# Bank of one transpose, a rounding piece and a search operation in a retention and FFN kernel

## The chip, the cores and the metric

The kernel runs on one core of one Trainium2 chip. The metric is device time in microseconds (us), the median of several executions; lower is better. The core has five engines with queues of their own: TensorE (PE, with its weight loads as PEld), VectorE (DVE), ScalarE (ACT), GpSimd (POOL) and SyncE (SP, which here only sends transfers).

## The reference

The input x has 4 sequences of 1024 tokens of 512 features, all float32. The computation is one layer in two parts, each added to its input after a layer norm on both sides:

```python
# part 1: x1 = x + layernorm(attn(layernorm(x)))
lam = clip(1.0 - 2.0 ** -beta, tiny, 1.0 - 1e-09)          # one per head, 16 heads of 32
q = (x @ Wq.T).reshape(B, L, 16, 32)
v = (x @ Wv.T).reshape(B, L, 16, 32)
ret = scan over time: state = lam * state + v_t
out = (q * ret).reshape(B, L, 512)
out = layernorm(out) * gamma + beta_ln
out = (out * silu(x @ Wg.T)) @ Wo.T
# part 2: out = x1 + layernorm(ffn(layernorm(x1))), inner width 1536
w_q = w.astype(float8_e4m3fn).astype(float32)              # for gate_w, up_w, down_w
gate = silu((x @ gate_wq) * gate_scale)
up = (x @ up_wq) * up_scale
out = ((gate * up) @ down_wq) * down_scale
```

The FFN weights are rounded to float8 and multiplied as float32.

## The kernel before

The 4096 tokens are cut into 8 blocks of 512 tokens (`TB`), a block into 4 tiles of 128 tokens. `Retention(t)` holds part 1 of block t, `Ffn` part 2. The FFN of a block runs in 12 steps (`NI`), one for each 128 of the 1536 inner columns. The main loop (`for t in range(NB)`, line 800) goes over blocks and, inside, over steps `i`. In iteration t it works on the FFN of block t (`f`, from `a`), on part 1 of block t + 1 (`b`, spread over the steps), on the beginning of block t + 2 (`n`, from step 4 or so), and on the end of the FFN of block t - 1 (`l`). All engine instructions are kept in the order in which the program names them, by the wrapper `InOrder` (its call is line 74, so every instruction of a profile shows line 74). Nothing reorders them: each engine runs its own list in that order, and semaphores between engines come from the tiles that instructions share.

[...] Two belong to the pool "pa" (products of part 1: pv, pq, pg, po, the means mu and var, and turns, named pt), two to "pf" (gate's and up's products in the FFN, pfg and pfu), four to "pd0" to "pd3" (the sums of down). A pool with two buffers hands them out in turn; a new tile has to wait until the last reader of the tile two places before it is done.

Three places matter.

Step 11, `if n and i == 11` (line 892). It holds the start of block t + 2 and the end of part 1 of block t + 1: `n.v(0)` makes pv (8 matmul instructions), `n.scan(0)` runs the scan over it on DVE (tile ret), `b.turn_x1n(3)` transposes the normalized x1 of the last tile by four matmuls into a bank (pt), and `b.upper_of(3)` and later `b.rest_of(3)` split it into two float32r parts, x1nT, one on ACT, one on DVE. Then `n.q(0)` makes pq (line 947), and `n.y_of(0)` multiplies it by ret on DVE. Tiles 0 to 2 are transposed otherwise, on DVE and by transfers through DRAM (`move_x1n`). The next iteration's `f.gate(0)` reads all of x1nT.

Rounding of the FFN weights. In float32, 18 pieces of 128 x 1024 elements are rounded during the prologue and block 0's FFN by `round_weights` (line 183), a generator; `rounds(n)` takes n of its operations. For each piece they are: a mask of the exponent on DVE (`unit`), two ACT instructions on the result, and an add and a subtract on DVE (`finish`). The add of a piece comes after the mask of the next one. The two ACT instructions are not sent with the mask, but at the next `units()`, which flushes all masks that are open; `rounds` calls it after each operation unless it is given `now=False`, and `finish` calls it when its own piece is still open. After its subtract, a piece frees its scratch, and the load of a later piece goes out on SP. In block 0's FFN three operations (one piece) run at step 0's beginning, three at step 4's beginning and three after `f.up` and `f.fuse` of each of the steps 0 to 7; the flush is before `f.up`, and in step 3 also right after `f.gate` and after each operation.

The variance of part 1's layer norm. In step 3 of an iteration, `b.halves()` splits the sum of y over the chunks into a float32r upper half on ACT and a lower half on DVE, `b.g_of(0)` makes pg, `b.mean()` averages both halves over the partitions on PE (mu), and `b.center_y()` subtracts mu from y on DVE, four instructions, squares the four results on ACT and sums the squares on POOL (sqsum). In step 4 the same halves are made of sqsum and averaged on PE (var), behind `b.g_of(1)`. Then come a square root on ACT and, after `f.up` and `f.fuse`, a reciprocal on DVE.

The search. `find_over` (line 228) is a generator of 24 ACT instructions that look for weights outside float8's range; each reads a quarter of one of the three weight matrices (128 x 1536) with one sign and writes a tile seen and its sum. From the seventh on, seen is one of two buffers that the halves and squares above use too. The table `look` (line 798) says how many run in each step of iteration t = 1: half of them, rounded down, after `f.gate`, and the others after `f.up` and `f.fuse`.

Of the kernel before, what the change touches and what calls it, by code (L numbers as in the profile page):

```python
# [23 lines left out]
def retention_ffn_sandwich(  # L24
# [190 lines left out]
    def units():  # L215

        while open_units:
            _, c = open_units.pop(0)
            act.activation(c, c, AF.Relu, bias=neg_low)
            act.activation(c, c, AF.Identity, scale=1.5 * 2.0**20, bias=low_unit)  # L220

    def rounds(n, now=True):
        for _ in range(n):
            next(rounding, None)
            if now:
                units()
# [71 lines left out]
    def turn(src, name, home="pa"):  # L298
        pt = homes[home].tile([P, NC, P], F32, tag=home, name=name)
        for c in range(NC):  # L300
            pe.transpose(pt[:, c, :], src[:, ts(c, P)], ident)
        return pt
# [14 lines left out]
    class Retention:  # L317
# [204 lines left out]
            )  # L522
            self.pt = {}

        def turn_x1n(self, s):
            self.pt[s] = turn(self.x1n.pop(s), f"pt1_{self.t}_{s}")

        def move_x1n(self, s):

# [160 lines left out]
    b = Retention(1)  # L690
# [104 lines left out]

    look = [2, 2, 2, 0, 2, 3, 3, 2, 2, 2, 2, 2]
    l = None
    for t in range(NB):  # L800
        f, n = Ffn(a), None
        for i in range(NI):
            if t > 0 and (t > 1 or i):
                (f if i else l).rest((i - 1) % NI)
            if t == 0 and i == 0:
                n = Retention(2)
                rounds(3, now=False)
            if t == 0 and i == 4:
                rounds(3, now=False)

            if l and i == 0:
# [25 lines left out]
            if t == 0 and i in (5, 6):  # L837
                n.norm_x(2 * i - 10, True)
                n.norm_x(2 * i - 9, True)
            if i == 3:  # L840
                units()
            for _ in range(look[i] // 2 if t == 1 else 0):
                next(search)

# [8 lines left out]
                l.stats(1)  # L853
            if b and i == 3:
                b.halves()
                b.g_of(0)
                b.mean()
                b.center_y()
                if t == 0:
                    n.stats(3)  # L860
                    n.rstd()
                    n.shift()
# [29 lines left out]
            if n and i == 11:  # L892
                n.v(0)
                n.scan(0)
                b.turn_x1n(3)
                b.upper_of(3)
            if t == 0:
                if i < 8:
# [66 lines left out]
        l, a, b = f, b, n  # L965
# [70 lines left out]
```

## Time and profile before

| | us |
|---|---|
| median of 3 runs (lowest, highest) | 1018.53 (1018.28, 1019.45) |
| the profiled execution | 1021.44 |
| its span, first to last instruction | 1019.7 |
| PE busy | 995.2 |
| DVE busy | 635.3 |
| ACT busy | 328.3 |
| POOL busy | 242.6 |
| PE matmuls of pfu, pfg and pd | 217.2, 190.2, 189.3 |
| PE matmuls of pq, pg, po | 115.5, 114.8, 114.5 |

The busy time of an engine is the sum over its instructions; the ends of matmuls are modelled, so that groups of matmuls overlap a little in the timeline. A row of the waits names the engine that stood still, the tile that it was about to write and the engine and tile that released it. A line of the timeline has the start from the beginning of the span, the length, the engine, the operation, output and inputs, how many instructions are merged in it, and in brackets the idle time before it with its releaser. Block numbers are not in the tile names: a place is found by its time. The FFN of block 0 begins at about 96 us, and an iteration of the loop takes about 123 us.

### The profile page before, as it was taken

The page shows a single profiled execution, that of the slowest core. Times are in us where ns is not written, and L with a number is a line of the kernel's source. Part 1 is how long each engine was busy: PE and PEld are TensorE (multiplying, and loading weights), DVE is VectorE, ACT ScalarE, POOL GpSimd, SP SyncE. Part 2 cuts the span into 40 slices and gives each one's busy share as a digit, 9 for nine tenths or more (in the row PEclk, how much of TensorE's full clock was granted, in tenths as well). Part 3 has the DMA queues.
Part 4 walks back from the last instruction along what each step waited for, and adds up shares of the span by engine and source line. Part 5 has one row for each costly group of instructions (what it writes and reads, how often), then busy time and mean ns, then how long its engine had stood idle before and what let it go on. Part 6 is the DMA issues. An engine that isn't in the chain of part 4 may idle for free.

```text
span 1019.7 us, 9800 instructions
## 1 busy us (share of the span) xinstructions
PE 995.2 (98%) x3502; PEld 654.1 (64%) x3502; DVE 635.3 (62%) x945; ACT 328.3 (32%) x489; POOL 242.6 (24%) x290
## 2 busy tenths in 40 slices
PE   8999989999999999999999999999999999999997
PEld 7454656656666666666666566665666656666885
DVE  4996888436767277663767537674476735747444
ACT  3546555523755124111231113211142111412222
POOL 1405131302222032221413114131141302313021
PEclk9999989999999999999999999999999999999999
DMA  8312212500216004250022501134020510103021
GB/s 283 120 62 88 98 63 82 135 11 21 62 56 171 1 22 144 78 150 1 21 73 83 134 1 58 35 114 104 0 83 31 129 68 1 42 21 123 2 83 41
DMA packets 62608, 73.79 MB, mean 72 GB/s; under 512 B 5856, under 2 KB 36320, under 8 KB 62560
## 3 DMA queue, kind: packets, MB, share of 16 engines
q1 hardware_dynamic: 60976, 72.24, 23.2%
q10 hardware_dynamic: 1584, 0.94, 0.4%
q8 instruction: 27, 0.44, 0.2%
q14 instruction: 21, 0.17, 0.1%
HBM read 43.53 MB, written 29.62 MB: 72 GB/s over the span
## 4 chain that ended last, share of the span: by engine, by line
PE 91%; DVE 4%; POOL 2%; ACT 1%; issue 1%; DMA 1%; ACTq 0%; POOLq 0%; DVEq 0%
PE pfu L74 17%; PE pfg L74 17%; PE pd L74 17%; PE pv L74 11%; PE pq L74 10%; PE po L74 10%; PE pg L74 9%; DVE ret L74 1%; DVE scr L74 1%; DMA x<-in_x 1%; POOL sqsum L74 1%; POOL x L74 0%; PE var L74 0%; POOL mv L74 0%; PE mu L74 0%
## 5 line engine op out<-in xcount | busy, mean ns | idle before, releaser
L74 PE MATMUL pfu<-x1nT,up_sb 128*128 128x512 f32 x768 | 217.2, 425 | 0.0
L74 PE MATMUL pfg<-x1nT,gate_sb 128*128 128x512 f32 x768 | 190.2, 390 | 1.1 <-ACT x1nT L74 0.7
L74 PE MATMUL pd<-down_sb,fuse 128*128 128x512 f32 x720 | 189.3, 405 | 0.0
L74 PEld LDWEIGHTS pfu<-x1nT,up_sb 128*128 128x128 f32 x768 | 145.6, 190 | 56.1 <-issue 28.9
L74 PEld LDWEIGHTS pfg<-x1nT,gate_sb 128*128 128x128 f32 x768 | 143.9, 188 | 31.7 <-DVE x1nT L74 1.0
L74 PEld LDWEIGHTS pd<-down_sb,fuse 128*128 128x128 f32 x720 | 136.0, 189 | 38.4 <-issue 10.8
L74 ACT CAST fuse<-gate 128x512 fp32r<-128x512 f32 x90 | 55.7, 619 | 274.9 <-DVE gate L74 274.9
L74 ACT ACTIVATE gate<-pfg,gs_sb 128x512 f32<-128x512 f32 x96 | 65.9, 687 | 234.3 <-PE pfg L74 234.2
L74 DVE SCALAR_TENSOR_TENSOR gate<-pfu,us_sb,gate 128x512 f32<-128x512 f32 x96 | 71.8, 748 | 106.3 <-PE pfu L74 106.2
L74 PE MATMUL pq<-xnT,wq_sb 128*128 128x512 f32 x256 | 115.5, 594 | 5.5 <-DVE ret L74 5.5
L74 PE MATMUL pv<-xnT,wv_sb 128*128 128x512 f32 (+1 forms) x280 | 114.8, 556 | 1.8 <-ACT xnT L74 1.8
L74 PE MATMUL pg<-xnT,wg_sb 128*128 128x512 f32 x256 | 114.8, 592 | 0.0
L74 PE MATMUL po<-wo_sb,y 128*128 128x512 f32 x256 | 114.5, 592 | 0.0
L74 POOL TENSOR_SCALAR mv<-mv 128x1 f32<-128x1 f32 (+1 forms) x77 | 19.8, 257 | 318.7 <-DVE mv L74 318.1
L74 PEld LDWEIGHTS pv<-xnT,wv_sb 128*128 128x128 f32 x280 | 52.8, 189 | 48.8 <-issue 43.4
L74 PEld LDWEIGHTS pq<-xnT,wq_sb 128*128 128x128 f32 x256 | 47.8, 189 | 55.9 <-issue 47.4
L74 DVE TENSOR_TENSOR fuse<-gate,fuse 128x512 fp32r<-128x512 f32 x90 | 79.4, 883 | 6.9 <-ACT fuse L74 6.9
L74 PEld LDWEIGHTS po<-wo_sb,y 128*128 128x128 f32 x256 | 48.4, 189 | 50.1 <-issue 47.7
L74 PEld LDWEIGHTS pg<-xnT,wg_sb 128*128 128x128 f32 x256 | 48.3, 189 | 49.6 <-issue 47.0
L74 POOL TENSOR_TENSOR x<-x,x1n 128x512 f32<-128x512 f32 x32 | 49.1, 1534 | 45.4 <-DVE x1n L74 35.5
L74 DVE TENSOR_TENSOR_SCAN ret<-lam,pv 128x512 f32<-128x512 f32 x16 | 19.5, 1219 | 54.4 <-PE pv L74 54.4
L74 DVE BATCH_NORM_STATS2 st<-x 128x6 f32<-128x512 f32 x64 | 43.6, 681 | 14.9 <-POOL x L74 11.2
(112 smaller groups left out, 926.1 us busy)
## 6 DMA issues: line engine op xcount, KB each, us to landing
kept<-x SPq DMA_DIRECT2D x32, 256.0 KB, 2.1
x<-kept SPq DMA_DIRECT2D x32, 256.0 KB, 4.0
x<-in_x SPq DMA_DIRECT2D x28, 256.0 KB, 4.1
out<-d SPq DMA_DIRECT2D x27, 256.0 KB, 2.0
xnT<-mx SPq DMA_DIRECT2D x24, 256.0 KB, 4.7
mxs<-xs SPq DMA_DIRECT2D x84, 64.0 KB, 1.8
x1n<-mxs SPq DMA_DIRECT2D x21, 256.0 KB, 2.6
mx<-xn SPq DMA_DIRECT2D x20, 256.0 KB, 2.2
```

The lines of the kernel that those rows point to most:

```text
L74: return lambda *args, **kwargs: tc.keep_in_program_order(op(*args, **kwargs))
```

## The change

It does three things.

1. `turn_x1n` takes the pool of its bank as an argument, and the call in step 11 under `if n` (iterations 0 to 5) uses "pf". The other calls keep "pa".
2. In block 0's FFN the three rounding operations from the beginning of step 4 go to step 3, behind `b.halves()`. The flush `units()` of step 3 (which stood behind `f.gate`, before `b.halves()`) goes to the same place, between them.
3. In `look`, step 4 has one operation in place of two, and step 7 three in place of two. In step 4 that is the one behind `f.gate`, in step 7 one more behind `f.fuse`.

```diff
-        def turn_x1n(self, s):
-            self.pt[s] = turn(self.x1n.pop(s), f"pt1_{self.t}_{s}")
+        def turn_x1n(self, s, home="pa"):
+            self.pt[s] = turn(self.x1n.pop(s), f"pt1_{self.t}_{s}", home)
...
-    look = [2, 2, 2, 0, 2, 3, 3, 2, 2, 2, 2, 2]
+    look = [2, 2, 2, 0, 1, 3, 3, 3, 2, 2, 2, 2]
...
             if t == 0 and i == 0:
                 n = Retention(2)
                 rounds(3, now=False)
-            if t == 0 and i == 4:
-                rounds(3, now=False)
...
-            if i == 3:
-                units()
             for _ in range(look[i] // 2 if t == 1 else 0):
                 next(search)
...
             if b and i == 3:
                 b.halves()
+                units()
+                if t == 0:
+                    rounds(3, now=False)
                 b.g_of(0)
                 b.mean()
                 b.center_y()
...
             if n and i == 11:
                 n.v(0)
                 n.scan(0)
-                b.turn_x1n(3)
+                b.turn_x1n(3, "pf")
                 b.upper_of(3)
```

`turn` is unchanged; it already takes the pool:

```python
    def turn(src, name, home="pa"):
        pt = homes[home].tile([P, NC, P], F32, tag=home, name=name)
        for c in range(NC):
            pe.transpose(pt[:, c, :], src[:, ts(c, P)], ident)
        return pt
```

## The prediction

> **What bounds the kernel now.** I read the busy table, the chain that ended last, the waits of TensorE, and then three stretches of the timeline. TensorE is the bound:
>
> ```profile
> PE 995.2 (98%) x3502; PEld 654.1 (64%) x3502; DVE 635.3 (62%) x945; ACT 328.3 (32%) x489; POOL 242.6 (24%) x290
> ...
> PE 91%; DVE 4%; POOL 2%; ACT 1%; issue 1%; DMA 1%; ACTq 0%; POOLq 0%; DVEq 0%
> ```
>
> So a change pays only where PE stands still. The waits (engine, waited for, us in total, times, longest) name two rows inside the loop, and the change touches both:
>
> ```profile
> PE pq L74 <- DVE ret L74: 5.5, 6, 1.0
> PE var L74 <- DVE half L74: 4.4, 2, 3.7
> ```
>
> The first sits in step 11 of blocks 0 to 5. Timeline, end of block 0 (start, length, engine, tile; in brackets the idle time before it):
>
> ```profile
> 204.19 0.60 PE L74 MATMUL pt<-ident,x1n 128*128 128x128 f32 x4
> ...
> 204.40 1.22 DVE L74 TENSOR_TENSOR_SCAN ret<-lam,pv 128x512 f32<-128x512 f32 x1 [2.61 <-PE pv L74]
> ...
> 205.67 3.70 PE L74 MATMUL pq<-xnT,wq_sb 128*128 128x512 f32 x8 [0.88 <-DVE ret L74]
> ```
>
> pv, pt and pq are consecutive users of the two "pa" banks: pq needs pv's bank, and the scan still reads it. The second row has one wait of 3.73 us in step 4 of block 0 and one of 0.68 us in step 4 of block 1:
>
> ```profile
> 131.49 1.22 DVE L74 TENSOR_TENSOR gate_sb<-scr,scr 128x1024 fp32r<-128x1024 f32 x1
> ...
> 132.08 0.61 ACT L74 CAST half<-sqsum 128x512 fp32r<-128x512 f32 x1
> ...
> 136.23 0.68 DVE L74 TENSOR_TENSOR half<-sqsum,half 128x512 fp32r<-128x512 f32 x1
> ...
> 136.97 0.80 PE L74 MATMUL var<-half,mean_r 128*128 128x512 f32 x1 [3.73 <-DVE half L74]
> ...
> 137.56 3.62 PE L74 MATMUL pfu<-x1nT,up_sb 128*128 128x512 f32 x8
> ```
>
> In block 0 the upper half was ready at 132.69, but DVE finished one weight piece, took the rest of fuse_3 and rounded another piece before the lower half. The pfu group behind it took 3.62 us where others take 1.98: the clock in one-microsecond windows is 0.64 in 136 to 137, 0.50 up to 143, 0.94 in 143 to 144.
>
> [...] after the 0.68 us gap (pfu 2.02 us) nothing fell. [...] during POOL's sqsum sums a scr sum took 2.29 us in place of 1.22. [...]
>
> **Part 1, the turn (blocks 0 to 5).** No instruction is added; two dependences change. pt takes the bank of pfg_11, read by ACT until 323.74 in block 1, where pt starts at 328.10: no wait. pq_0 takes the bank of po_3, read last at 320.28 to 321.09: no wait. The gain of a site is the time from pt's end to pq's end, less eight unstalled f32 matmuls, 3.43 us by the chain: 209.37 - 204.79 - 3.43 = 1.15 us in block 0. In blocks 1 to 5 it is 1.26, 1.15, 1.21, 1.15 and 1.21 [...]. The sum is 7.13. In block 6 pt is followed by pd without a wait, and pd ends 1.86 after pt where eight unstalled take 1.83: some 0.03 per site remains. I take **-7.0**, bounds -5.5 (the bare idle) and -7.2.
>
> What is late next? gate_0 of the next block needs all of x1nT; in block 1 DVE finishes it at 331.04, and gate_0 starts at 335.08, so 333.8 when all moves up: 2.8 us of cover, 2.8 to 3 in blocks 2 to 5 too (577.19 against 581.23, less 1.2). up_0 takes pt's bank, free from that same DVE instruction, and starts at 339.92. v(1) takes pv_0's bank, free at 329.64, wanted at 335.7. y_of(0) on DVE follows pq, 1.2 earlier, and DVE is idle there (2.39 before it). If the cover failed, every microsecond beyond 2.8 would stall PE one for one.
>
> **Part 2, the search operation (block 1).** ACT's order was gate_4, seen, half[...]:
>
> ```profile
> 259.98 1.56 ACT L74 ACTIVATE seen<-gate_sb,neg_max 128x1536 fp8e4<-128x1536 f32 x1
> 261.44 0.19 ACT L74 ACTIVATION_READ_ACCUMULATOR seen<-gate_sb,neg_max 128x1 f32 x1
> 261.53 0.61 ACT L74 CAST half<-sqsum 128x512 fp32r<-128x512 f32 x1
> ```
>
> Without the seen pair the cast can start at 260.22, when POOL's sqsum (256.04 plus 4.14) is done; it ends at 260.83. The lower half then waits for the first of POOL's two d sums (260.14 to about 261.5) and ends near 262.1; that it gets in between two POOL sums is seen at 257.00, where two DVE operations took 2.04 us during POOL's three sqsum sums. pg_1's matmuls end at 262.78, so nothing waits. From var's start to pfu's took 264.03 - 262.22 = 1.81; in step 3, mu without a wait takes 253.75 - 252.88 = 0.87. Gain **-0.9**; bounds -0.95 and 0 (if the half waits for both d sums, until 263.08, it ends where it did). rstd stays at 264.73 behind the table load (263.44 plus 1.28), but reciprocal follows gate_4 on DVE, which moves up with pfu.
>
> In step 7 the operation (1.57 plus 0.19) goes behind the one at 294.14; gate_8 on ACT moves from 296.39 to 297.6. Its reader on DVE starts at 301.72, and pfg_8's bank is wanted at 303.26: covered by 3 us. xs of step 8 (298.88) takes the buffer of the added seen, finished at 297.6: covered by 1.2 us, and behind it by x1nT's slack. Cost 0.
>
> **Part 3, the rounding piece (block 0).** It moves three DVE instructions (0.68, 1.22, 1.22) ahead of center_y in step 3, and with them the flushes of ACT. Its load is out at 115.81 and lands in 3.6, before 122.8. The instruction that SP sends after each piece (piece 15's load) goes out near 127 in place of 132.74, earlier; nothing queues behind it.
>
> DVE is free at 122.26, the half of ysum is ready since ACT no longer flushes first (cast at 119.8 instead of 122.03): lower half 122.26, piece 122.86 to 125.9, center_y at 125.86 where it was at 123.94, 1.9 later. mu comes 0.4 earlier, which PE only spends waiting for var. POOL's first sqsum sum ends 3.4 after center_y (ACT's last sq started at 127.35 against 123.94): that sq at 129.27.
>
> Now ACT's new order decides: sq, flush of piece 13, fuse_3, **flush of piece 14**, gate_4, half. Flush 14 ran after rstd before (138.39); now it stands ahead of the half. By start-to-start times in the trace: sq 0.56, flush 2.23, fuse 0.54, flush 2.23, gate 0.57: half at 129.27 + 6.13 = 135.40, done at 136.0. DVE, free by 135.4, makes the lower half until 136.7; var's second matmul starts at about **136.8**, where it was 136.97. So the piece leaves DVE's queue ahead of the half, but ACT's queue gets as long as DVE's was: the 3.7 us wait stays, now mostly for the upper half. Gain 0.2. PE starts again with var's first matmul at 136.05, 0.9 earlier, so the half-clock stretch may end a little earlier. I take **-0.4**; bounds -4 ([...] 6 us at half speed cost 3.0) and +3 [...]. rstd comes at 138 in place of 137.80 and is needed at 141.9.
>
> **Sum.** -7.0 - 0.9 - 0.4 = **-8.3**. The profiled execution took 1021.44 with a span of 1019.7: its span becomes 1011.4. The median is 2.9 under the profiled time; its waits should be the same, so 1018.53 - 8.3 = **1010.2**.
>
> **Rivals.**
> - *The clock falls differently in block 0.* [...] 3.0 more go: 1007.2. For: PE resumes 0.9 earlier by a first matmul. Against: idle stays about 3.7. The reverse gives 1013.2.
> - *Part 3 works as its DVE side suggests*: the half directly after sqsum (132.3), wait and slow clock gone: 3.73 + 3.0 in place of 0.4, near 1003.9. [...]
> - *The turn only exchanges its wait*: half of 7.0, for instance because gate_0 waits for x1nT, 1013.7. Against: 2.8 us of cover in each block.
> - *Slower*: ACT takes x1nT's tile 2 only when its DMA has landed (574.11 in block 3, ACT idle 4.11). If that landed over 2.8 + 8.3/6 = 4.2 us later in all six blocks, gate_0's stall would eat everything; at 5 us the time is 1023. Against: nothing on SP ahead of it is moved there.
> - *The change doesn't do what it says*: the order of instructions shows it does, ACT's flushes included.
>
> **How the numbers follow.** Main case 0.68 (1008.8 to 1011.6); the clock better 0.13, worse 0.05; part 3 as hoped 0.03; an exchanged wait 0.07; no change 0.02; slower 0.02. Cutting the ends leaves 1006.8 to 1012.9. Below 0.2% (2.0 us) a measurement cannot tell a change; faster 0.96, same 0.02, slower 0.02.
>
> **What would show it.** Right: the row pq waiting for ret is gone; in each of blocks 0 to 5 pq ends some 3.5 after pt; only one gap before var is left, 3.5 to 4.2 us in block 0, with ACT's flush of piece 14 between fuse_3 and gate_4; center_y there near 125.9. Wrong: a new row for pfg or pt in step 11, or var's gap in block 0 under 2 us or over 5.

## The result, and the profile after

| | before | changed |
|---|---|---|
| median of 6 runs (lowest, highest), us | 1018.78 (1018.28, 1019.45) | 1010.83 (1010.38, 1011.77) |
| the profiled execution, us | 1021.44 | 1010.72 |
| its span, us | 1019.7 | 1008.9 |
| PE idle (span less busy), us | 24.5 | 17.5 |

The ratio is 0.9923 with a 95% interval of 0.9910 to 0.9936, so 7.95 us less by the medians. The two profiled executions differ by more, 10.8 us in span, and two things in that are not the change. Before starts its first pv at 11.16 us, the changed kernel at 9.62, because the first loads of x landed at different times (the one on the way to that pv took 5.67 us in before and 4.11 in the changed kernel). And the half-clock stretch in block 0 is of different length in the two (below): from var's second matmul to the pfg behind it takes 6.85 us in before (136.97 to 143.82) and 5.59 in the changed kernel (135.06 to 140.65), a difference of 1.3 us. So places are compared here by distances inside an execution, not by their times from the start.

The busy table and the chain by engine, of the changed kernel, answer to the first two lines of before: TensorE is still the bound.

```profile
PE 991.4 (98%) x3502; PEld 652.7 (65%) x3502; DVE 633.8 (63%) x945; ACT 328.0 (33%) x489; POOL 241.2 (24%) x290
...
PE 91%; DVE 3%; POOL 2%; ACT 2%; DMA 1%; issue 0%; ACTq 0%; SPq 0%; POOLq 0%; DVEq 0%
```

TensorE's waits (us in total, times, longest) that answer to the two rows of before:

```profile
PE var L74 <- ACT half L74: 3.6, 1, 3.6
...
PE pv L74 <- DMA xnT<-mx: 0.2, 1, 0.2
PE var L74 <- DVE half L74: 0.2, 1, 0.2
```

The row of pq waiting for ret (5.5 us, 6 times) is gone. Of the 4.4 us in which var waited for the half of VectorE, 0.2 are left, but 3.6 have come in which it waits for the half of ScalarE. A small row is new: a pv that waits for the transfer of xnT.

The timeline of step 11 at the end of block 0, changed kernel: pq now starts right behind the turn (201.48, where the turn starts at 201.04), while the scan still reads pv's bank, that is, pv's buffer of 128 x 512 float32.

```profile
201.04 0.60 PE L74 MATMUL pt<-ident,x1n 128*128 128x128 f32 x4
201.24 1.22 DVE L74 TENSOR_TENSOR_SCAN ret<-lam,pv 128x512 f32<-128x512 f32 x1 [2.61 <-PE pv L74]
201.48 3.60 PE L74 MATMUL pq<-xnT,wq_sb 128*128 128x512 f32 x8
```

And steps 3 and 4 of block 0, changed kernel, from center_y to pfu_4:

```profile
124.20 2.47 DVE L74 TENSOR_TENSOR y<-y,mu 128x512 f32<-128x512 f32 x4
...
127.60 0.63 ACT L74 ACTIVATE sq<-y 128x512 f32<-128x512 f32 x1 [0.80 <-POOL sqsum L74]
...
128.14 1.13 ACT L74 ACTIVATE scr<-scr,neg_low 128x1024 f32<-128x1024 f32 x1
...
129.31 1.15 ACT L74 ACTIVATE scr<-scr,low_unit 128x1024 f32<-128x1024 f32 x1
...
130.36 0.60 ACT L74 CAST fuse<-gate 128x512 fp32r<-128x512 f32 x1
...
130.87 1.14 ACT L74 ACTIVATE scr<-scr,neg_low 128x1024 f32<-128x1024 f32 x1
...
132.05 1.15 ACT L74 ACTIVATE scr<-scr,low_unit 128x1024 f32<-128x1024 f32 x1
...
133.10 0.67 ACT L74 ACTIVATE gate<-pfg,gs_sb 128x512 f32<-128x512 f32 x1
133.67 0.60 ACT L74 CAST half<-sqsum 128x512 fp32r<-128x512 f32 x1
...
134.31 0.69 DVE L74 TENSOR_TENSOR half<-sqsum,half 128x512 fp32r<-128x512 f32 x1 [0.74 <-ACT half L74]
134.33 0.50 PE L74 MATMUL var<-half,mean_r 128*128 128x512 f32 x1 [3.58 <-ACT half L74]
...
135.06 0.52 PE L74 MATMUL var<-half,mean_r 128*128 128x512 f32 x1 [0.22 <-DVE half L74]
...
135.39 3.57 PE L74 MATMUL pfu<-x1nT,up_sb 128*128 128x512 f32 x8
```

ScalarE runs without a pause from the last square to the upper half: flush of piece 13, fuse_3, flush of piece 14, gate_4, half. VectorE is now the one that waits (0.74 us). The last line shows half clock again behind the gap (pfu took 3.57 us, in step 3 of the same block 2.00). How long it lasted is read from windows of one microsecond (start and end, length, busy time and count of PE, PEld, DVE, ACT, POOL, then the granted clock, the share of the DMA engines and GB/s). These are the first and the last window of the stretch, in before:

```profile
136.00:137.00 1.00, 0.03 (x1) 0.03 (x1) 0.91 (x2) 0.00 (x0) 0.37 (x1) 0.64 0.00 0
...
143.00:144.00 1.00, 1.00 (x5) 0.77 (x5) 1.00 (x1) 0.00 (x0) 0.00 (x0) 0.94 0.00 0
```

and in the changed kernel:

```profile
135.00:136.00 1.00, 0.94 (x3) 0.81 (x4) 0.00 (x1) 1.00 (x1) 0.00 (x0) 0.70 0.81 285
...
138.00:139.00 1.00, 1.00 (x4) 0.80 (x3) 0.00 (x0) 0.00 (x0) 0.00 (x0) 0.59 0.00 0
```

A clock of 0.64 over one microsecond is 0.36 / 0.5 = 0.72 us at half speed. All windows between show 0.50, those around 1.00. So the stretch was, as an estimate from these windows, 0.72 + 6 + 0.12 = 6.8 us in before and 0.60 + 2 + 0.82 = 3.4 us in the changed kernel. It began at 136.28 in before, ahead of the matmul that ended the gap (136.97), and at 135.40 in the changed kernel, behind that matmul (134.33).

### The profile page after: what moved, and what is told of

The parts are those of the page before. It is cut to its first block, busy times and chain, and to the rows that moved or that the text cites. A ratio compares the mean times of both kernels' runs of the same rounds, so it can differ in the third digit from the quotient of the medians.

```text
span 1008.9 us, 9809 instructions
## 1 busy us (share of the span) xinstructions
PE 991.4 (98%) x3502; PEld 652.7 (65%) x3502; DVE 633.8 (63%) x945; ACT 328.0 (33%) x489; POOL 241.2 (24%) x290
## 4 chain that ended last, share of the span: by engine, by line
PE 91%; DVE 3%; POOL 2%; ACT 2%; DMA 1%; issue 0%; ACTq 0%; SPq 0%; POOLq 0%; DVEq 0%
PE pfu L74 17%; PE pfg L74 16%; PE pd L74 16%; PE pv L74 11%; PE pq L74 10%; PE pg L74 10%; PE po L74 10%; DVE scr L74 1%; POOL sqsum L74 1%; DMA xnT<-mx 1%; POOL x L74 1%; POOL mv L74 0%; DVE st L74 0%; PE var L74 0%; ACT scr L74 0%
## 5 line engine op out<-in xcount | busy, mean ns | idle before, releaser
L74 PEld LDWEIGHTS pd<-down_sb,fuse 128*128 128x128 f32 x720 | 135.4, 188 | 38.2 <-issue 10.8
```

Of the source, the lines that this page charges most:

```text
L74: return lambda *args, **kwargs: tc.keep_in_program_order(op(*args, **kwargs))
```

## The experiments

Times are compared with runs of before on the same chip: median 1020.0 (41 runs) for the first four, 1019.54 (9 runs) for the last four. What a run is said to be "less" than before comes from its ratio, which is not the quotient of the two medians; the medians themselves differ by 7.4, 1.4, 1.0 and 8.2 us in the first four, and by 7.6 with pv in "pf".

### Each part alone

The first three kernels are before with one hunk of the change. The turn, in blocks 0 to 5:

```diff
-                b.turn_x1n(3)
+                b.turn_x1n(3, "pf")
```

> Part 1 alone: only the turn of the last x1n tile goes to the pf bank. Bank theory (pq waits for pv's bank, nothing else is late behind it): 7.0 us faster than before (6.5 to 7.2), ratio 0.9931; the row pq waiting for ret is gone, both var waits stay. Exchange theory (the wait goes to gate_0 or to the next pv): half of that or less, with a new row for pfg or pv in step 11.

Measured: 1012.6 us (1011.79 to 1014.92, 5 runs), ratio 0.9930 (0.9914 to 0.9946), 7.1 us less. The row pq waiting for ret is gone; TensorE's wait for the halves is that of before:

```profile
PE var L74 <- DVE half L74: 4.4, 2, 3.7
```

The bank theory holds and the exchange theory falls. The loop shows it block by block. The distance from one pt to the next, in us, is one iteration of TensorE:

| kernel | blocks 0-1 | 1-2 | 2-3 | 3-4 | 4-5 |
|---|---|---|---|---|---|
| before | 123.91 | 123.30 | 122.90 | 122.99 | 122.90 |
| turn alone | 122.78 | 122.04 | 121.78 | 121.78 | 122.39 |
| changed | 121.78 | 122.04 | 121.78 | 121.78 | 122.25 |

Four of the five differences of the turn alone are 1.13, 1.26, 1.12 and 1.21 us. The fifth is 0.51: there a pv of the next block waited for xnT's transfer (0.4 us in this run). The sixth distance, from block 5 to 6, is 120.51 us in before and 119.32 in both others, so the turn alone gives 6.4 us along this profile.

The search operation:

```diff
-    look = [2, 2, 2, 0, 2, 3, 3, 2, 2, 2, 2, 2]
+    look = [2, 2, 2, 0, 1, 3, 3, 3, 2, 2, 2, 2]
```

> Part 2 alone: one search operation from step 4 to step 7 of block 1. Theory: 0.9 us faster (0.7 to 1.0), ratio 0.9991, which timing may not tell from no change; the profile has only the block 0 wait in the row var waiting for half, and var to pfu in block 1 takes 0.87 us in place of 1.81. Rival: the half on VectorE waits for both of GpSimd's sums, and the gap of 0.68 us stays.

Measured: 1018.63 us (1017.32 to 1021.59, 21 runs), ratio 0.9990 (0.9983 to 0.9998), 1.0 us less. TensorE's timeline in step 4 of block 1, in before:

```profile
262.22 0.79 PE L74 MATMUL var<-half,mean_r 128*128 128x512 f32 x1
...
264.03 2.02 PE L74 MATMUL pfu<-x1nT,up_sb 128*128 128x512 f32 x8
```

and in this run:

```profile
259.46 1.03 PE L74 MATMUL var<-half,mean_r 128*128 128x512 f32 x2
260.33 1.98 PE L74 MATMUL pfu<-x1nT,up_sb 128*128 128x512 f32 x8
```

From var to pfu it takes 0.87 us in place of 1.81: both matmuls of var run without a gap. No new wait of TensorE came in step 7. In the table above it is the first column's step from 122.78 to 121.78.

The rounding piece:

```diff
-            if t == 0 and i == 4:
-                rounds(3, now=False)
...
-            if i == 3:
-                units()
...
                 b.halves()
+                units()
+                if t == 0:
+                    rounds(3, now=False)
                 b.g_of(0)
```

> Part 3 alone: one rounding piece of block 0 from step 4 to step 3. Theory of ScalarE's queue (the flush of piece 14 now stands ahead of the upper half): within 1 us of before unless the clock falls differently, then up to 2 us faster; the profile shows a gap of 3.3 to 4 us before var, released by the upper half on ScalarE. Theory of VectorE alone (the rounding was what held the lower half): 6 us faster, no gap over 1 us.

Measured: 1019.02 us (1017.96 to 1020.12, 21 runs), ratio 0.9988 (0.9981 to 0.9995), 1.2 us less. The gap stays, released by ScalarE:

```profile
134.41 0.60 ACT L74 CAST half<-sqsum 128x512 fp32r<-128x512 f32 x1
...
135.05 0.69 DVE L74 TENSOR_TENSOR half<-sqsum,half 128x512 fp32r<-128x512 f32 x1 [0.74 <-ACT half L74]
135.07 0.50 PE L74 MATMUL var<-half,mean_r 128*128 128x512 f32 x1 [3.59 <-ACT half L74]
```

The theory of VectorE alone, 6 us and no gap over 1 us, falls.

Parts 1 and 2 together, without part 3:

> Parts 1 and 2 without part 3. If the parts add up: 7.9 us faster than before, ratio 0.9922, so within 1 us of the changed kernel. If part 3 is worth what VectorE's side suggests: only 7.9 of the changed kernel's gain would be missing nothing, so this run and the changed kernel must differ by 4 us or more for that theory to stand.

Measured: 1011.79 us (1011.12 to 1012.71, 5 runs), ratio 0.9918 (0.9905 to 0.9932), 8.4 us less. That can't be told from the changed kernel, so the parts add up as far as these intervals tell, and nearly everything is in the first two.

### Another exchange of banks

Before, with pv in a "pf" bank and the turn where it was:

```diff
-                n.v(0)
+                n.v(0, "pf")
                 n.scan(0)
```

> Before, with another exchange of banks: pv of step 11 goes to a pf bank and the turn stays in pa, so that pq takes a bank that the scan does not read. Bank theory: the same gain as the turn alone, 7.0 us (6.5 to 7.2). Rival, that the order or length of the turn itself matters: a different gain, by 2 us or more.

Measured: 1011.99 us (1011.37 to 1012.98, 5 runs), ratio 0.9922 (0.9910 to 0.9935), 8.0 us less; its interval overlaps that of the turn alone. The distances from pt to pt are 122.78, 122.04, 121.78, 121.78 and 121.78, and 119.31 to block 6: 7.0 us in all. So what took the wait away is that pq does not take the bank that the scan reads; whether pt or pv moved made no difference to it. The two differ in block 5, where pv did not wait here.

### What holds var in block 0

The changed kernel, with the flush of piece 14 back behind rstd:

```diff
-                    rounds(3, now=i == 3)
+                    rounds(3, now=False)
```

> The changed kernel, but the rounds after step 3's gate and up do not flush, so that piece 14's two ScalarE instructions run behind rstd in step 4 again; VectorE's order is that of the changed kernel. Theory of ScalarE's queue: the upper half comes 2.2 us earlier, the lower half is then bound by VectorE (its rounding ends near 133.0), var's second matmul 0.8 us earlier; 0.8 us faster than the changed kernel, up to 2.5 if the clock no longer falls. Rival, that ScalarE's flush is not what holds var: no change, and the first matmul of var waits as long as in the changed kernel.

Measured: 1009.74 us (1009.33 to 1011.09, 4 runs), ratio to before 0.9901 (0.9888 to 0.9915). The changed kernel beside it (last in this section) took 1011.99, so 2.2 us less. Timeline, this run:

```profile
131.26 0.60 ACT L74 CAST half<-sqsum 128x512 fp32r<-128x512 f32 x1
...
131.92 0.49 PE L74 MATMUL var<-half,mean_r 128*128 128x512 f32 x1 [1.38 <-ACT half L74]
...
133.30 0.68 DVE L74 TENSOR_TENSOR half<-sqsum,half 128x512 fp32r<-128x512 f32 x1
134.04 0.50 PE L74 MATMUL var<-half,mean_r 128*128 128x512 f32 x1 [1.62 <-DVE half L74]
```

The upper half no longer waits for the flush, and VectorE, still rounding, holds the lower one: the gap is split into 1.38 and 1.62 us. Var's second matmul comes 0.8 us earlier than in the changed kernel (39.04 against 39.85 us in the table of distances below), as the theory of ScalarE's queue said. The other 1.4 of the 2.2 us can't be put down to the order: the clock still fell, for 3.4 us, and the mean granted clock was 0.997 in three of these four executions but 0.995 in four of the five beside it.

The changed kernel with the second piece of step 3 also behind the halves, those of step 4, and with the flush of the first piece behind the upper half:

```diff
             if b and i == 4:
                 b.halves()
+                units()
+                if t == 0:
+                    rounds(3, now=False)
                 b.g_of(1)
...
-            units()
+            if t > 0 or i != 3:
+                units()
             f.up(i)
...
-                if i < 8:
-                    rounds(3, now=i == 3)
+                if i < 8 and i != 3:
+                    rounds(3, now=False)
```

> The changed kernel, with step 3's second rounding piece also behind the halves of step 4 and the flushes of both pieces behind the upper halves. Theory: both engines reach the halves when sqsum is ready, var's second matmul some 3.0 us earlier, gap before var under 1 us, no fall of the clock: 4.5 us faster than the changed kernel (3 to 6.5), near 1006.3. Rival: the piece comes back as lateness of VectorE in steps 4 to 7, with a new wait of TensorE for y, pfu or a rounded weight, and less than 2 us is gained.

Measured: 1006.96 us (1006.57 to 1007.43, 4 runs), ratio to before 0.9873 (0.9858 to 0.9889), 5.0 us less than the changed kernel beside it. Timeline of step 4 in block 0:

```profile
130.45 0.62 ACT L74 CAST half<-sqsum 128x512 fp32r<-128x512 f32 x1 [1.29 <-POOL sqsum L74]
...
131.10 0.69 DVE L74 TENSOR_TENSOR half<-sqsum,half 128x512 fp32r<-128x512 f32 x1 [1.81 <-ACT half L74]
...
131.12 0.51 PE L74 MATMUL var<-half,mean_r 128*128 128x512 f32 x1 [0.60 <-ACT half L74]
...
131.85 0.50 PE L74 MATMUL var<-half,mean_r 128*128 128x512 f32 x1 [0.22 <-DVE half L74]
```

and the window of 16 us behind the place:

```profile
132.00:148.00 16.00, 15.48 (x59) 10.97 (x60) 14.37 (x15) 11.05 (x14) 0.65 (x2) 1.00 0.22 67
```

ScalarE now waits for sqsum (1.29 us) and VectorE for ScalarE's half (1.81 us), the gap is 0.60 and 0.22 us, and the clock stays at 1.00. The rounding that was put off does come back, in one new wait of 0.5 us of pfg for gate_5 on ScalarE; that is small. From var's second matmul to the next pfg it is 3.98 us without half clock, where before took 6.85 and the changed kernel 5.59: a half-clock stretch cost 2.9 us when it was long and 1.6 when it was short. The gain over the changed kernel is then, as an estimate from these figures, 2.97 us of var's second matmul, plus 1.6 or 2.9, less 0.5: 4.1 or 5.4 us, with 5.0 measured. This version beats both kernels.

The changed kernel once more, on the chip of these runs:

> The changed kernel once more, beside the two made from it: near 1010.8.

Measured: 1011.99 us (1009.93 to 1012.91, 5 runs), ratio 0.9918 (0.9905 to 0.9931). That is 1.2 us over what was expected; before is 0.8 us higher on this chip too (1019.54 against 1018.78), so the ratio is nearly that of the first runs (0.9923).

## Why the prediction was right

It gave 1010.2 us (8.3 less); measured are 1010.83 and 7.95 less. Along the two profiles, leaving the clock out, the six distances from pt to pt give 7.56 us for the turn and the search operation, and var's second matmul 0.37: 7.9 in place of 8.3. The missing 0.4 is about what a wait for xnT took that the prediction did not have; the timing, 6.5 to 9.2 us less by its interval, does not resolve that. By its steps:

- **The turn, -7.0.** The working per site holds to hundredths. From pt's end to pq's end it is 3.44 us in block 0 after the change where it was 4.58, so 1.14 against the 1.15 of the sum, and the iterations of the following blocks became shorter by 1.26, 1.12 and 1.21 us, the terms of the sum being 1.26, 1.15 and 1.21. The idle time of the wait's row (5.5 us) would have been too little; what makes it 7 is that the group behind a wait ended later by more than the idle time shown (1.15 to 1.26 us against 0.88 to 1.00). The runs show the size of that difference, not its cause. The cover of gate_0 held: no wait of pfg for x1nT is new.
- **A cover that was not named.** The prediction looked at who uses the banks and x1nT next, and at one more transfer, but not at xnT's, which pv waits for at the head of the same step. In before, the last of that transfer's four parts is issued at 810.5 in block 5, transfers of this tile took up to 6.0 us from there, and pv starts at 816.76: as an estimate from these, some 0.3 us of cover. In the six profiles with the turn in "pf" the slowest took 6.4 to 6.8 us. In four of them pv waited 0.2 to 0.5 us in block 5, in the other two it started 0.25 us late (2.06 us behind the start of the pfu in front of it, where before has 1.81) with no wait listed. In the changed kernel:

```profile
807.16 3.67 PE L74 MATMUL pv<-xnT,wv_sb 128*128 128x512 f32 x8 [0.23 <-DMA xnT<-mx]
```

This wait is the difference between 122.25 and 121.78 in the table: about 0.5 us of the gain lost. Why the transfer is slower there is not settled, and so neither is whether the turn's bank causes it. In the four profiles without the turn in "pf" the slowest took 6.0 to 6.2 us, and the schedule gives no reason: in all ten, mx's last transfer goes out 2.05 to 2.07 us ahead of xnT's first part, and the next four behind it at 1.95 or 1.96 us.

- **The search operation, -0.9.** Right in place and size: 1.0 us by timing, 0.94 us by the timeline (1.81 to 0.87). In the changed kernel the lower half took 1.54 us (256.58 to 258.12), begun during the first of POOL's two d sums, and ended before pg_1 did.
- **The rounding piece, -0.4 with the gap staying.** The step that decided it, ScalarE's order, is what the trace shows, instruction by instruction. As distance from block 0's first pfg matmul (96.75 in before) to var's second matmul:

| kernel | first pfg | var's second | distance |
|---|---|---|---|
| before | 96.75 | 136.97 | 40.22 |
| piece alone | 95.92 | 135.80 | 39.88 |
| changed | 95.21 | 135.06 | 39.85 |
| late flush | 95.00 | 134.04 | 39.04 |
| both behind | 94.97 | 131.85 | 36.88 |

The gain of the matmul itself was put at 0.2 us and is 0.37: center_y started 0.1 us earlier than worked out (28.99 behind the first pfg, not 29.11), and ScalarE's row of instructions behind it was some 0.1 us shorter. The other 0.2 of the -0.4 was the author's estimate, for a half-clock stretch that ends a little earlier. That is not how it went: a stretch took 3.4 or 6.8 us (next point), so that 0.4 and 0.37 meet is in part luck. Timing of the piece alone shows 1.2 us (0.5 to 1.9), more than either. Part of that lies in the clock: six of before's 41 executions had a mean granted clock under 0.995, none of the piece's 21. At 0.996 the two kernels differ by 0.3 us (means of 11 and 9 executions), at 0.995 by 0.75 (17 and 9), at 0.997 by 0.4 the other way (7 and 3). Whether this order makes low clocks rarer is not shown.

- **The clock, where the bounds were put.** It fell in each of the eight profiles with a gap of 3.58 to 3.73 us, and behind the split gap of the late flush (1.38 and 1.62 us). The mean granted clock from 132 to 148 us is 0.79 in three of the ten profiles, 0.89 in six and 1.00 in the one with both pieces behind the halves. By narrower windows (one microsecond for before, the changed kernel and the late flush, four for the others) and with 0.50 within a stretch, its length is, as an estimate, 6.8 us in the three, 3.4 in the six and 0 in the one. Both longer values were seen with the changed kernel (3.4 and, run once more, 6.8) and with the old order of step 4 (6.8 in before and with pv in "pf", 3.4 with the turn alone, the search operation alone and both). So the length isn't fixed by the kernel. It went with the moment of the fall: by the same windows the clock fell 0.4 to 0.9 us ahead of the matmul that ended the gap in the three profiles with 6.8 us, and 0.4 to 1.5 us behind it in the six with 3.4 us. The second part, worth 1.3 us between before and the changed kernel, comes or goes between executions.
- **The rivals.** The wait that is only exchanged and the slower case did not come (the 0.5 us of xnT's transfer aside), and the one in which part 3 works as VectorE's side suggests was shown false by the piece alone, and true in what it promised by the version with both pieces behind the halves: var 3.0 us earlier than in the changed kernel, and no half clock. That version moves the flushes behind the halves as well, which is what ScalarE's order calls for.

## What to carry to other kernels

When two pool buffers serve three products in a row, the third waits for the reader of the first: here pq for the scan, six times, 5.5 us in all. A bank borrowed from a pool that had one free there removed the wait. What the wait costs is read as the distance from end to end, which was more than the idle time shown (1.15 to 1.26 us a time against 0.88 to 1.00). When work is moved ahead of a wait, list the order of every engine that the moved step feeds: here the VectorE instructions left the queue ahead of the half, their ScalarE flush entered the other half's queue, and the gap of 3.73 us became one of 3.58. Before a wait is taken away, look also at the transfers that the same instruction needs: one of them had some 0.3 us of cover, and in four of the six profiles with the turn in "pf" pv waited for it, 0.2 to 0.5 us.

## What the runs showed of the hardware

In the late flush, a gap split into 1.38 and 1.62 us, with one matmul of 0.49 us between, was followed by a half-clock stretch of 3.4 us. In the version with both pieces behind the halves, gaps of 0.60 and 0.22 us were followed by none: the clock is 1.00 from 132 to 148 us. In before, none followed the gap of 0.68 us in block 1 either: the clock is 1.00 in each microsecond from 262 to 269. How long a gap has to be for the clock to fall is not shown by these runs; that it might stay up in block 0 of the changed kernel, or that an earlier start of TensorE would end the stretch earlier, were the author's estimates.

The changed kernel's gap was followed by 3.4 us at half clock in one execution (gap 3.58 us), where the clock fell 1.1 us after TensorE went on, and by 6.8 us in another (gap 3.60 us), where it fell 0.4 us before. What sets the moment of the fall is not shown.
